# A four-layer convolution network: x2 made chunk by chunk, and the first two chunks' 7x7 products written to DRAM ahead of their factors

## The chip, the core and the metric

The kernel runs on one core of one Trainium2 chip. The metric is the device time of one execution in microseconds. The kernel before took 5029.39 us (median of 3 runs, 5021.53 to 5036.27). The engines are TensorE (PE, with its weight loads as PEld), VectorE (DVE), ScalarE (ACT), GpSimd (POOL) and SyncE (SP, which here only issues DMAs). Each runs its own queue of instructions in order, and waits for the others by semaphores.

## What is computed

The input is x of shape 4 x 384 x 64 x 64, float32. Four layers follow each other, each as x = x + layer(...). The change lies in the third and the fourth:

```
# layer 2, its end ("h1", "h2", token mixing done before; batch norms over batch and pixels)
h1 = gelu(bn(w1 @ tok));  h2 = bn(w2 @ h1);  ch = tok + h2
x2 = x + gate * ch + (1 - gate) * x_in

# layer 3, on v = groupnorm(x2) over 32 groups of 12 channels
avg, top = v.mean((2, 3)), v.max((2, 3))
x_w  = gelu(avg @ w_avg.T + b_avg + top @ w_max.T + b_max)      # one number per batch, channel
xr   = x_w * w_mix                                             # 7 x 7 taps per batch, channel
Nx   = norm(xr) / (norm(xr).mean over channels + 1e-6)
kern = gamma * xr * Nx + beta
out  = x2 + depthwise_conv7x7(v, kern)
```

For one batch and channel, kern is a factor times w_mix, plus beta. So out is x2, plus (gamma Nx x_w) times a 7x7 convolution of v with w_mix, plus beta times a 7x7 box sum of v. The convolution with w_mix is linear: the factor can be put on v before it, or on its result after it.

## The kernel before

The 384 channels are three chunks of 128 (j = 0, 1, 2); an image of a chunk is 128 partitions x 4096 floats, 2 MB. The phases follow each other: A to D make layers 0, 1 and the start of 2; E (part of `phase_ef`) makes the tokens and the first matrix product of layer 2, batch by batch in 4 blocks of 1024 pixels; F makes h2 by the second product; G (`phase_g`) does x2 and layer 3.

**E and F.** For each block, E loads three token tiles (L1363), scales them (L1364), multiplies (L1379) and stores the result, and the running sum "wx", to DRAM. Two token tiles rotate over two buffers; the third lies in a large buffer `z_`, in slot `i % 3` of 1024 floats. F loads, applies gelu (L1422), multiplies (L1435), copies to SBUF and stores h2 to DRAM, but for the last batch, whose h2 stays in `z_`. Statistics of the batch norms are gathered on DVE over all batches at the end (L1406, L1450).

**G, x2.** `x2_of(b)` makes one batch: for its three chunks (order 1, 2, 0) and quarters of 1024, ACT scales h2 into PSUM (L1614), DVE adds it to wx (L1615), ACT squares for the variance (L1617), DVE takes the maximum (L1618). Chunks 1 and 2 are stored to DRAM. Then come the factors of that batch: group norm, two small products on PE (L1636, L1653), gelu. Beside the next batch's x2, `first_chunk` makes chunk 0's strips and boxes of this one. Batch 3 comes first.

**G, strips and products.** `to_strips` (from SBUF, L1678) or `half_strips` (from DRAM, 64 channels at a time, L1555, L1561) apply the factor and norm, transpose on PE and lay the rows in `z`. `conv7(j, c0)` takes 8 channels: it loads weights (L1702), forms four Toeplitz blocks, two of three on DVE and one of three on POOL (L1709), multiplies on PE (L1722), adds the "rest" tile (L1730), which was loaded from DRAM (L1704), and stores the output (L1731). 16 such calls make a chunk, 48 in all.

**G, boxes.** `boxes(j, b, x)` adds beta times the box sum to x2: row sums on POOL (L1766, L1768) and DVE (L1769 to L1783), transposes and a product on PE (L1789, L1795), with an ACT copy between (L1791), and the scaled add into x2 on DVE (L1797). The result, x2 plus box, is the "rest" (L1801) that conv7 adds. So chunk j's boxes have to be done before its products; chunk 1's run beside chunk 0's products, chunk 2's beside chunk 1's, and none beside chunk 2's.

The order in which generators are advanced is written by hand in `phase_g`; a scheduler of the language then sets the final order on each engine. Buffers rotate by tag: two for weights, three each for "rest" and for x tiles, four for Toeplitz blocks.

Of the kernel before, what the change touches and what calls it, by code (L numbers as in the profile page):

```python
# [226 lines left out]
class _Builder:  # L227
    def __init__(self, ctx, tc, ins, out):
# [25 lines left out]
        self.rest = [self.dram.tile([P, 32, B, P], F32, tag=f"rest{j}", name=f"rest_{j}") for j in range(NJ)]  # L254
# [72 lines left out]
    def over_batches(self, name, mv):  # L327

        nc = self.nc
        st = self.sm([P, NJ, 6], f"{name}_st")  # L330
        m = self.sm([P, NJ, 2], f"{name}_m")
        for j in range(NJ):
            nc.vector.bn_stats(st[:, j, :], mv[:, j, :, 0])
            nc.vector.bn_aggr(m[:, j, :], st[:, j, :])
        within = self.sm([P, NJ], f"{name}_w")
        nc.vector.tensor_reduce(within, mv[:, :, :, 1], AX.X, ALU.add)
        var = self.sm([P, NJ], f"{name}_v")
        nc.vector.scalar_tensor_tensor(var, within, 1.0 / B, m[:, :, 1], ALU.mult, ALU.add)
        return m[:, :, 0], var
# [215 lines left out]
    def stats_tile(self, name):  # L555
        return self.sm([P, NJ, 8, 6], name, 1)
# [418 lines left out]
    def open_strips(self, ctx):  # L975
# [6 lines left out]
        self.h2_last = self.z_[:, 0 : NJ * N].rearrange("p (j n) -> p j n", n=N)  # L982
# [318 lines left out]
    x2_order = 1, 2, 0  # L1301

    def phase_ef(self, strips):
        tc, nc = self.tc, self.nc
        with ExitStack() as ctx:
# [47 lines left out]
            st = ep.tile([P, 6, B * 8, 6], F32, tag="h_st", name="h_st")  # L1353
            sums = cp.tile([P, NJ, B, 4], F32, tag="wx_sum", name="wx_sum")
            for b in range(B):
                for i in range(4):
                    blk = slice(i * 1024, (i + 1) * 1024)
                    t01 = io.tile([P, NJ - 1, 1024], F32, tag="tok", name="e_tok")
                    at = i % 3 * 1024
# [44 lines left out]
            mv = self.sm([P, 6, 2], "h_mv")  # L1404
            for o in range(6):
                nc.vector.bn_aggr(mv[:, o, :], st[:, o].rearrange("p a b -> p (a b)"))  # L1406
            a1, c1 = self.bn_scale_shift("bn_h", mv[:, :, 0], mv[:, :, 1], self.vec("cm_g1"), self.vec("cm_b1"))
# [8 lines left out]
            for b in range(B):  # L1416
                for i in range(4):
# [7 lines left out]
                    if b == B - 1 and 0 < i:  # L1425
                        j = self.x2_order[i - 1]
                        nc.sync.dma_start(self.x2_ahead[i - 1], self.wx[b][:, j])
                    for j in range(NJ):
                        out = self.h2_last[:, j, blk]
                        if b < B - 1:  # L1430
                            out = io.tile([P, 1024], F32, tag="x", name="f_h2")
# [12 lines left out]
                        if b < B - 1:  # L1444
                            nc.gpsimd.dma_start(self.h2[b][:, j, blk], out)
                for j in range(NJ):
                    nc.vector.bn_aggr(mvb[:, j, b], st2[:, j, 8 * b : 8 * b + 8].rearrange("p a b -> p (a b)"))
            mv = self.sm([P, NJ, 2], "h2_mv")
            for j in range(NJ):
                nc.vector.bn_aggr(mv[:, j, :], st2[:, j].rearrange("p a b -> p (a b)"))  # L1450
            a2, c2 = self.bn_scale_shift("bn_h2", mv[:, :, 0], mv[:, :, 1], self.vec("cm_g2"), self.vec("cm_b2"))
# [15 lines left out]
    def phase_g(self):  # L1467
# [8 lines left out]
        with ExitStack() as ctx:  # L1476
# [17 lines left out]
            sq = self.sm([P, NJ, 49], "mix_sq", 1)  # L1494
            nc.vector.tensor_mul(sq.rearrange("p j k -> p (j k)"), self.vec("w_mix"), self.vec("w_mix"))
# [3 lines left out]
            for k in ("a_s", "a_b", "b_s"):  # L1499
                setattr(self, k, cp.tile([P, NJ, B], F32, tag=k, name=k))  # L1500

            self.off = cp.tile([P, NJ, B, 3], F32, tag="off", name="off")


            self.z = self.z_[:, 0 : P * 136].rearrange("p (c k b) -> p c k b", k=34, b=B)
            nc.gpsimd.memset(self.z_[:, P * 136 :], 0.0)
            behind = iter(())
            for n, b in enumerate((B - 1, *range(B - 1))):
                for x in self.x2_of(b):
                    next(behind, None)  # L1510
                for _ in behind:
                    pass
                if n == 0:
                    nc.gpsimd.memset(self.z[:, :, 0], 0.0)
                behind = self.first_chunk(b, x)
            for _ in behind:
                pass
            self.pair_scales(cp)

            for j in range(NJ):  # L1520
                boxes = self.boxes_of(j + 1)
                for half in range(2):
                    strips = self.half_strips(j + half, 1 - half) if 0 < j + half < NJ else iter(())
                    for n in range(8):
                        self.conv7(j, 64 * half + 8 * n)
                        next(strips, None)
                        for _ in range(3 + n % 2):
                            next(boxes, None)
                    for _ in strips:
                        pass  # L1530
                for _ in boxes:
                    pass

    def pair_scales(self, pool):

        self.a_pair = pool.tile([P, 2, 2, NJ, 2], F32, tag="a_pair", name="a_pair")
        for half in range(2):
            for u in range(2):
                for k, v in enumerate((self.a_s, self.a_b)):
                    self.nc.gpsimd.dma_start(  # L1540
                        self.a_pair[64 * u : 64 * u + 64, k, half],
                        v[64 * half : 64 * half + 64, :, u::2],
                    )

    def half_strips(self, j, half):

        nc = self.nc
        for pair in range(2):
            for part in range(3):
# [10 lines left out]
                s, b = (self.a_pair[:, k, half, j, pair : pair + 1] for k in range(2))  # L1560
# [14 lines left out]
    def first_chunk(self, b, x):  # L1575
        yield from self.to_strips(0, b, x)
        yield from self.boxes(0, b, x)

    def boxes_of(self, j):
        if j < NJ:  # L1580
            for b in range(B):
                yield from self.boxes(j, b, self.load_x2(j, b))

# [8 lines left out]
    def x2_of(self, b):  # L1592


        nc = self.nc
        mv = self.sm([P, NJ, 2], "gn_mv")
        mx = self.sm([P, NJ], "max")
        for j in self.x2_order:
# [233 lines left out]
```

## Time and profile before

| what | value |
|---|---|
| median of 3 runs | 5029.39 us |
| the profiled execution | 5034.98 us |
| its span, first to last instruction | 5033.2 us |
| PE, DVE, ACT, POOL busy over the span | 92%, 54%, 42%, 15% |
| mean granted TensorE clock | 0.95 |
| moved by DMA | 723.30 MB |
| end of the last h2 product (F) | 4222.1 us |
| first 7x7 product | 4513.6 us |

The page cuts the span in 40 slices and gives each a digit: the busy share in tenths. "PEclk" is the TensorE clock granted, in tenths. A row of a group reads: line, engine, operation, written <- read, shape, count, then busy us and mean ns of one, then idle time just before and what ended it. A row of the table of stages gives, for each stretch of time, the busy time of PE, PEld, DVE, ACT and POOL with the number of instructions, then the clock, the mean busy share of the 16 DMA engines, and GB/s.

In phase G, DVE's largest groups are the Toeplitz blocks and the x2 work; ACT waits for DMA-loaded strips and for PE; the longest waits of PE lie between 4227 and 4510 us, for DVE's group norm and factors.

### The profile page before, as it was taken

To read this page: it belongs to the slowest core of one execution; us is meant where nothing else is said; L and a number is where in the kernel's file an instruction comes from. 1 tells how busy PE (TensorE), PEld (TensorE's weight loads), DVE (VectorE), ACT (ScalarE), POOL (GpSimd) and SP (SyncE) were. 2 spreads that over 40 slices of the span, in tenths; PEclk is the share of its full clock that TensorE was granted. 3 is DMA by queue.
4 is the path that set the end of the run, shared out by engine and by line. 5 is a ranking of instruction groups with operands and counts; after the bars stand their busy time and mean duration, and the time that the engine had idled before them with its cause. 6 is when DMAs were issued, how large, how long until landed. Compare 5 with 4: busy or idle time off the path is not lost. (4 is left out here: it accounts for less than half of the span.)

```text
span 5033.2 us, 47996 instructions
## 1 busy us (share of the span) xinstructions
PE 4607.7 (92%) x17875; PEld 2614.2 (52%) x17875; DVE 2729.0 (54%) x4480; ACT 2108.7 (42%) x2811; POOL 762.8 (15%) x568
## 2 busy tenths in 40 slices
PE   5999999999999999999988999699999996569999
PEld 2333444334443444435467888344444443558999
DVE  5322455644656445565867778544421114767775
ACT  4444344554445444445345665311133334652320
POOL 1000000000000000000035555000000000135543
PEclk8999999999999999999989999799999997569999
DMA  5210211110111101113259999766664433757876
GB/s 167 72 48 29 84 57 60 65 59 33 68 63 65 52 32 63 63 61 100 89 162 286 290 293 296 255 239 248 238 238 150 150 134 136 255 181 229 235 214 193
DMA packets 344919, 723.30 MB, mean 144 GB/s; under 512 B 22011, under 2 KB 172390, under 8 KB 337766
## 3 DMA queue, kind: packets, MB, share of 16 engines
q1 hardware_dynamic: 283032, 477.56, 30.4%
q0 software_dynamic: 33152, 136.60, 7.2%
q10 hardware_dynamic: 28494, 105.99, 5.4%
q8 instruction: 144, 2.36, 0.2%
q14 instruction: 97, 0.79, 0.0%
HBM read 432.48 MB, written 287.57 MB: 143 GB/s over the span
## 5 line engine op out<-in xcount | busy, mean ns | idle before, releaser
L749 PE MATMUL av<-probs,vt 128*128 128x512 f32 x2048 | 964.6, 606 | 0.0
L720 ACT ACTIVATE probs<-sc_s 128x1024 f32<-128x1024 f32 x512 | 500.9, 1021 | 788.1 <-PE av L749 781.5
L749 PEld LDWEIGHTS av<-probs,vt 128*128 128x128 f32 x2048 | 370.3, 192 | 468.1 <-issue 461.0
L1154 PE MATMUL conv_m<-toep,z 128*128 128x256 f32 x2304 | 522.2, 386 | 11.0 <-DVE toep L1135 6.8
L945 DVE SCALAR_TENSOR_TENSOR acc<-band,vecs,acc 128x512 f32<-128x512 f32 x708 | 496.7, 746 | 45.8 <-POOL band L906 40.0
L1435 PE MATMUL h_m<-f_h,cm_w_t 128*128 128x512 f32 x1152 | 496.4, 594 | 7.9 <-ACT f_h L1422 7.9
L1154 PEld LDWEIGHTS conv_m<-toep,z 128*128 128x128 f32 x2304 | 440.5, 193 | 73.1 <-DVE z L1087 4.9
L1379 PE MATMUL h_s<-e_tok,cm_w_t 128*128 128x512 f32 x768 | 367.4, 602 | 5.5 <-DVE e_tok L1364 5.5
L1435 PEld LDWEIGHTS h_m<-f_h,cm_w_t 128*128 128x128 f32 x1152 | 219.4, 191 | 284.9 <-issue 273.8
L1135 POOL TENSOR_TENSOR toep<-w,band 128x1536 f32<-128x1536 f32 x94 | 323.8, 3445 | 285.7 <-PE conv_m L1154 244.7
L1722 PE MATMUL conv_m<-toep,z 128*128 128x128 f32 x3072 | 366.4, 278 | 0.1
L1722 PEld LDWEIGHTS conv_m<-toep,z 128*128 128x128 f32 x3072 | 357.1, 194 | 0.5 <-issue 0.5
L712 PE MATMUL sc_s<-q,k 32*128 32x512 f32 x2048 | 297.8, 650 | 22.5 <-ACT probs L720 22.0
L868 PE MATMUL t_m<-w_in_t,xb 128*128 128x384 f32 x768 | 276.9, 495 | 2.7 <-DVE coef L885 1.6
L1386 ACT COPY e_h<-h_s 128x1024 f32<-128x1024 f32 x96 | 97.2, 1012 | 421.4 <-PE h_s L1379 421.4
L782 PE MATMUL proj_m<-xm,w_proj_t 128*128 128x512 f32 x576 | 265.9, 600 | 5.0 <-DVE xm L735 3.5
L1379 PEld LDWEIGHTS h_s<-e_tok,cm_w_t 128*128 128x128 f32 x768 | 148.1, 193 | 192.6 <-issue 185.6
L789 DVE SCALAR_TENSOR_TENSOR x_res<-proj_m,bn_c,x_res 128x512 f32<-128x512 f32 x96 | 71.8, 748 | 319.5 <-PE proj_m L782 316.5
L1388 DVE BATCH_NORM_STATS2 h_st<-e_h 128x6 f32<-128x512 f32 x192 | 123.4, 685 | 194.9 <-ACT e_h L1386 194.9
L1443 DVE BATCH_NORM_STATS2 h_st<-f_h 128x6 f32<-128x512 f32 x72 | 49.8, 694 | 323.1 <-ACT f_h L1442 323.1
L868 PEld LDWEIGHTS t_m<-w_in_t,xb 128*128 128x128 f32 x768 | 142.7, 191 | 138.8 <-issue 59.6
L1379 PE MATMUL h_s<-z,cm_w_t 128*128 128x512 f32 x384 | 198.0, 599 | 12.6 <-DVE z L1364 12.6
(369 smaller groups left out, 6285.1 us busy)
## 6 DMA issues: line engine op xcount, KB each, us to landing
d<-d_o ACTq DMA_DIRECT2D x96, 512.0 KB
c_d<-d SPq DMA_DIRECT2D x96, 512.0 KB
hid<-e_h ACTq DMA_DIRECT2D x16, 3072.0 KB
f_h<-hid SPq DMA_DIRECT2D x16, 3072.0 KB
x_in<-in_x SPq DMA_DIRECT2D x96, 256.0 KB
x_res<-in_x SPq DMA_DIRECT2D x32, 768.0 KB
xa<-x_res POOLq DMA_DIRECT2D x32, 768.0 KB, 3.7
xa_in<-xa SPq DMA_DIRECT2D x32, 768.0 KB
```

Source lines behind the costliest of these rows:

```text
L712: nc.tensor.matmul(s[:, g], lhsT=k4[32 * g : 32 * g + 32, c], rhs=q[i][32 * g : 32 * g + 32], start=True, stop=True,)
L720: nc.scalar.activation(p[:, h * 1024 : (h + 1) * 1024], s[:, 2 * h : 2 * h + 2].rearrange("p a b -> p (a b)"), AF.Exp, scale=0.25,)
L749: nc.tensor.matmul(av, lhsT=vt[:, 4 * c + v, :], rhs=p[:, v * 512 : (v + 1) * 512], start=c == 0 and v == 0, stop=c == 7 and v == 3,)
L782: nc.tensor.matmul(m, lhsT=self.w_proj[:, j, o * P : (o + 1) * P], rhs=xm[:, j], start=j == 0, stop=j == NJ - 1,)
L868: nc.tensor.matmul(m[:, 0:C], lhsT=xb[:, j], rhs=self.w_in[:, j, :], start=j == 0, stop=j == NJ - 1,)
L945: nc.vector.scalar_tensor_tensor(out, src(j, k), w, done, ALU.mult, ALU.add)
L1135: eng.tensor_tensor(t, self.w53[:, at : at + 192].rearrange("p (m n) -> p m n", n=8).unsqueeze(2).to_broadcast([P, 24, 8, 8]), band.rearra ...
L1154: nc.tensor.matmul(m[:, c * 256 : (c + 1) * 256], lhsT=self.z_[:, at : at + P], rhs=t[:, 12 * c + 4 * i : 12 * c + 4 * i + 4].rearrange("p ...
L1379: nc.tensor.matmul(s[:, v, :], lhsT=w1[:, j, o * P : (o + 1) * P], rhs=t[j][:, v * 512 : (v + 1) * 512], start=j == 0, stop=j == NJ - 1,)
L1388: nc.vector.bn_stats(st[:, o, 8 * b + 2 * i + v, :], h[:, o, v * 512 : (v + 1) * 512])
L1435: nc.tensor.matmul(m, lhsT=w2[:, o, j * P : (j + 1) * P], rhs=h[:, o, v * 512 : (v + 1) * 512], start=o == 0, stop=o == 5,)
L1722: nc.tensor.matmul(m[:, ch * P : (ch + 1) * P], lhsT=self.z_[:, at : at + P], rhs=t[:, 8 * c + 2 * i : 8 * c + 2 * i + 2].rearrange("p m a ...
```

## The change

It makes x2 for chunk 0 of all batches first, then its strips, scaled by 1 and with the group mean taken off (the mean is known ahead of x2 from the sums). Then chunk 0's products run and are stored raw, without their factor; beside them x2 of chunks 1 and 2 is made (in `phase_g` two or three steps of `x2` for each conv7). When all x2 are there, `factors` makes the factors of all batches at once. Chunk 1's strips are unscaled too and its products raw; chunk 2's strips carry the factor, as before. All boxes run beside the products of chunks 1 and 2, in the order (2, all batches), (0, all), (1, all), 4 or 5 steps for each conv7; for chunks 0 and 1 the box loads the raw products and adds them, times the factor, and stores the output itself. Chunk 0's x2 is now stored to DRAM and loaded back as well.

Besides: all h2 go to DRAM, the last batch's too; E's third token tile rotates over the batches; the statistics of both batch norms are kept by batch and joined by `over_batches`, which is rewritten; some small tiles move to other pools.

```diff
+        self.rest = self.dram.tile([P, 32, B, P], F32, tag="rest", name="rest")
+        self.raw = [self.dram.tile([P, P, P], F32, tag=f"raw{j}", name=f"raw_{j}") for j in range(NJ - 1)]
...
@@ over_batches
+        nc.vector.tensor_reduce(mean, mv[:, :, :, 0], AX.X, ALU.add)
+        nc.vector.tensor_scalar(mean, mean, 1.0 / B, None, ALU.mult)
+        d = self.sm([P, n, B], f"{name}_d")
+        nc.vector.tensor_sub(d, mv[:, :, :, 0], mean.unsqueeze(2).to_broadcast([P, n, B]))
+        nc.vector.tensor_mul(d, d, d)
+        nc.vector.tensor_add(d, d, mv[:, :, :, 1])
+        nc.vector.tensor_reduce(var, d, AX.X, ALU.add)
+        nc.vector.tensor_scalar(var, var, 1.0 / B, None, ALU.mult)
@@ phase_ef
-                    at = i % 3 * 1024
+                    at = (4 * b + i) % 3 * 1024
...
+                for o in range(6):
+                    nc.vector.bn_aggr(hmv[:, o, b], st[:, o, 8 * b : 8 * b + 8].rearrange("p a b -> p (a b)"))
...
-                        nc.sync.dma_start(self.x2_ahead[i - 1], self.wx[b][:, j])
+                        nc.sync.dma_start(self.x2_ahead[i - 1], self.wx[i - 1][:, 0])
...
-                        if b < B - 1:
-                            nc.gpsimd.dma_start(self.h2[b][:, j, blk], out)
+                        nc.gpsimd.dma_start(self.h2[b][:, j, blk], out)
@@ phase_g
+            self.group_means()
             behind = iter(())
+            for b in range(B):
+                for x in self.x2_of(0, b):
                     next(behind, None)
                 for _ in behind:
                     pass
+                behind = self.to_strips(0, b, x)
             for _ in behind:
                 pass
+            self.pair_scales(1)
...
+            x2 = others(*(self.x2_of(j, b) for j in (1, 2) for b in range(B)))
+            boxes = others(*(self.boxes(j, b) for j, b in ((2, 0), (2, 1), (2, 2), (2, 3), (0, 0), (0, 1), (0, 2), (0, 3))))
+            boxes1 = others(*(self.boxes(1, b) for b in range(B)))
             for j in range(NJ):
                 for half in range(2):
                     strips = self.half_strips(j + half, 1 - half) if 0 < j + half < NJ else iter(())
                     for n in range(8):
                         self.conv7(j, 64 * half + 8 * n)
                         next(strips, None)
+                        for k in range(5):
+                            if j == 0 and (k < 2 or k == 2 and n % 2):
+                                next(x2, None)
+                            if j == 1 or j == 2 and (k or n % 2):
+                                next(boxes, None)
                     for _ in strips:
                         pass
+                if j == 0:
+                    for _ in x2:
+                        pass
+                    self.factors()
+                    self.pair_scales(2)
+                if j == 1:
+                    boxes = others(boxes, boxes1)
...
+    def group_means(self):
+        m = self.over_groups("gn_pg", self.mean2)
+        nc.vector.tensor_copy(self.gm, m)
+        for i, k in enumerate((-6.0, -7.0, 2.0)):
+            nc.vector.tensor_scalar(self.off[:, :, :, i], self.gm, k, None, ALU.mult)
+        nc.gpsimd.memset(self.s_s, 1.0)
+        nc.vector.tensor_scalar(self.s_b, self.gm, -1.0, None, ALU.mult)
...
+    def factors(self):
...
+        nc.vector.tensor_mul(self.a_s, gx, r)
+        nc.vector.tensor_mul(self.b_s, over(self.vec("beta")), r)
+        nc.vector.tensor_copy(self.s_s[:, 2], self.a_s[:, 2])
+        nc.vector.scalar_tensor_tensor(self.s_b[:, 2], self.gm[:, 2], -1.0, self.a_s[:, 2], ALU.mult, ALU.mult)
@@ x2_of(j, b), the quarter
+            h = self.gw_p.tile([P, 1024], F32, tag="w7", name="g_h2", bufs=3)
+            nc.sync.dma_start(h, self.h2[b][:, j, sl])
+            for v in range(2):
+                m = self.pm("x2_m")
+                part = slice(q * 1024 + v * 512, q * 1024 + v * 512 + 512)
+                nc.scalar.activation(
+                    m, h[:, v * 512 : v * 512 + 512], AF.Identity, bias=at(self.g0), scale=at(self.gh)
+                )
+                nc.vector.tensor_add(x[:, part], x[:, part], m)
+            nc.scalar.activation(h, x[:, sl], AF.Square, bias=at(self.neg2), accum_out=self.x2_var[:, j, b, q : q + 1])
+            nc.vector.tensor_reduce(self.x2_max[:, j, b, q : q + 1], x[:, sl], AX.X, ALU.max)
+            yield None
+        nc.gpsimd.dma_start(self.scratch["x2"][b][j], x)
@@ conv7
-        nc.sync.dma_start(o, self.rest[j][c0 : c0 + 8].rearrange("c y b n -> (y b) c n"))
+        if j == NJ - 1:
+            nc.sync.dma_start(o, self.rest[c0 : c0 + 8].rearrange("c y b n -> (y b) c n"))
...
+        if j < NJ - 1:
+            nc.scalar.copy(of, m)
+            nc.scalar.dma_start(self.raw[j][:, c0 : c0 + 8], o)
+            return
         nc.vector.tensor_add(of, of, m)
         nc.sync.dma_start(self.out[j][:, c0 : c0 + 8], o)
@@ boxes
-            h = self.gw_p.tile([P, 16 * W], F32, tag="w7", name="box_7")
+            h = self.gw_p.tile([P, 16 * W], F32, tag="w7", name="box_7", bufs=3)
...
+            if j < NJ - 1:
+                d = self.gt_p.tile([P, 1024], F32, tag="rest", name="in_raw", bufs=3)
+                nc.sync.dma_start(
+                    d.rearrange("p (y n) -> p y n", n=P),
+                    self.raw[j].rearrange("(y b) c n -> c y b n", b=B)[:, 8 * part : 8 * part + 8, b],
+                )
+                xp = x[:, part * 1024 : (part + 1) * 1024]
+                nc.vector.scalar_tensor_tensor(xp, d, self.a_s[:, j, b : b + 1], xp, ALU.mult, ALU.add)
```

## The prediction

> **What bounds the kernel now.** I read the page first, then a table of stages, then the groups of the last stages by form. The page: TensorE (PE) is busy nearly everywhere, except in slices 34 to 36.
>
> ```profile
> span 5033.2 us, 47996 instructions
> ...
> PE   5999999999999999999988999699999996569999
> ...
> DVE  5322455644656445565867778544421114767775
> PEclk8999999999999999999989999799999997569999
> ```
>
> One digit is 126 us. The 6, 5, 6 lie between about 4150 and 4530 us; the granted clock falls there too. The table of stages (columns: PE, weight load, DVE, ACT, POOL busy, then clock, DMA share, GB/s) cuts this end in three: x2 with factors and chunk 0's strips and boxes; the 7x7 of chunks 0 and 1; the 7x7 of chunk 2.
>
> ```profile
> 4227.00:4510.00 283.00, 146.66 (x704) 132.83 (x705) 195.47 (x361) 188.12 (x264) 62.44 (x63) 0.57 0.62 223
> 4510.00:4890.00 380.00, 350.80 (x2962) 343.68 (x2963) 289.17 (x341) 105.73 (x187) 190.58 (x122) 0.97 0.76 225
> 4890.00:5033.00 143.00, 138.13 (x1237) 137.88 (x1235) 84.20 (x73) 14.96 (x19) 54.61 (x27) 1.00 0.65 198
> ```
>
> For 283 us no engine is the bound: DVE 69%, ACT 66%, PE 52% at a clock of 0.57. Then PE is the bound (92%, 97%), and DVE has room: 24% free in the second row, 41% in the third. The change moves 7x7 products (PE) into the first row and spreads DVE's boxes into the last. The first 7x7 matmul starts at 4513.6 us by the rows of its line, the last ends at 5028.2 by the chain. The groups by form, from 4215 us, give the prices:
>
> ```profile
> L1722 PE MATMUL conv_m<-toep,z 128*128 128x128 f32 x3072 | 366.4, 278 | 0.1
> ...
> L1709 DVE TENSOR_TENSOR toep<-wmix,band_p 128x1024 f32<-128x1024 f32 x129 | 155.5, 1215 | 42.6 <-PE conv_m L1722 35.7 <-issue 3.8 <-DMA wmix<-in_mix_t 1.9
> ...
> L1615 DVE TENSOR_TENSOR x<-x,x_m 128x1024 f32<-128x1024 f32 x48 | 57.4, 1214 | 13.6 <-ACT x_m L1614 12.3 <-DMA x<-wx 1.3
> L1618 DVE TENSOR_REDUCE x_max<-x 128x1 f32<-128x1024 f32 x48 | 57.3, 1211 | 0.0
> ...
> L1791 ACT COPY ht<-ht_m 128x512 f32<-128x512 f32 x96 | 56.1, 585 | 112.3 <-PE ht_m L1789 112.2
> ...
> L1797 DVE SCALAR_TENSOR_TENSOR in_x<-box_m,b_s,in_x 128x512 f32<-128x512 f32 x64 | 47.8, 747 | 22.0 <-PE box_m L1795 21.4
> ```
>
> The chain at the end shows 64 of these matmul records in 7.15 us, 0.1117 each: a chunk's 1024 cost 114 us of PE at full clock, 343 for three.
>
> **Phase E, a small part that is all on the path.** PE is the bound there, and the timeline shows it idle once at each change of batch:
>
> ```profile
> 3335.13 2.07 PE L1379 MATMUL h_s<-z,cm_w_t 128*128 128x512 f32 x2 [3.91 <-DVE z L1364]
> ...
> 3465.22 1.12 PE L1379 MATMUL h_s<-z,cm_w_t 128*128 128x512 f32 x2 [3.77 <-DVE z L1364]
> ...
> 3595.67 1.69 PE L1379 MATMUL h_s<-z,cm_w_t 128*128 128x512 f32 x2 [4.88 <-DVE z L1364]
> ```
>
> The third token chunk lives in slot i % 3: blocks 3 and 0 of adjoining batches take the same slot, so the load waits for the matmuls before it. With (4b + i) % 3 it has two blocks (62 us) of lead, as inside a batch, where no wait shows. Phase E ran from 3200.9 to 3717.8; 1152 records at 0.429 are 494; its cold start lost 3; 19.6 remain, 12.6 of it the idle above and the rest matmuls at half clock behind it. I take -19 (from -12.6 to -19.6). Statistics by batch add small DVE work under PE; at both ends of phase F one 0.96 us aggregate gives way to seven operations of some 0.16: nothing, within 0.5.
>
> **To the first x2.** The last h2 matmul, 4222.1, moves to 4203. Before, the first x2 used data kept in SBUF; now h2 is read back. Four DMAs of 0.4 us stand before that load on SP; a 512 KB store landed in 3.0 us; that ends about when the coefficients do (5.6 us after the last matmul). ACT starts at 4210; +3 at worst. The twelve extra h2 stores on POOL (12 x 3.0 = 36 us if bare) hide under batch 3's matmuls, as those of the other batches do.
>
> **Stage 1: x2 and strips of chunk 0 alone.** ACT carries it. x_m in halves of 512 costs 1.19 - 0.43 = 0.76 (0.43 is the 1024 copy's 1.01 less the 512 copy's 0.585). A tile: 8 x 0.76 + 4 x 1.33 (square and its accumulator) = 11.4; its strips 3 x 1.52 + 3 x (1.13 + 0.88) = 10.6. Four tiles: 88 us. DVE, beside it: 4 x (8 x 0.75 + 4 x 1.21) + 12 x 1.09 = 56. Before, ACT ran at 95 to 100% in such stretches (4240 to 4260): 93 us, the 7x7 starts at 4303 instead of 4513.6.
>
> **Stage 2: chunk 0's 7x7 beside the other eight tiles of x2.** PE: 114 + 6 strips x 1.2 = 121. DVE: 43 x 1.215 + 8 x 10.8 + 6 x 1.09 = 146. ACT: 8 x 11.4 + 16 raw copies x 1.01 + 16 DMA issues x 0.37 + 6 strips x 2.67 = 129. DMA: x2 in (6 tiles, two come early), h2 in (8) and x2 out (8), at 2.1 MB each 46 MB; raw out 8; weights 4; strips and first boxes 6: 64 MB. The full 10 us windows of the old x2 stage:
>
> ```profile
> 4290.00:4300.00 10.00, 4.69 (x21) 4.10 (x22) 7.57 (x14) 9.19 (x11) 1.97 (x3) 0.50 1.01 396
> ...
> 4370.00:4380.00 10.00, 5.05 (x39) 4.14 (x37) 9.00 (x9) 9.00 (x14) 0.55 (x1) 1.00 0.82 288
> ...
> 4390.00:4400.00 10.00, 7.23 (x34) 6.74 (x32) 8.99 (x21) 6.87 (x12) 2.69 (x2) 0.50 0.96 376
> ```
>
> At some 370 GB/s 64 MB need 173 us: DMA is the bound, not an engine. Two waits are new: ACT's raw copy waits for PE, with x_m and the squares of the next tile queued behind it (two product banks give it one step, 11 us, of slack); the weights' loads on SP wait for a finished step, with the h2 loads behind them (three h2 buffers cover some 17 us). I take 185; 155 if more is prefetched and DVE binds, 215 at 300 GB/s. The clock is a place where a rule speaks against the change. In the middle row PE was half busy and kept 1.00. The Trainium skill (TensorE: Matmul & The Clock Gate, "HAM oscillation") says that idle gaps over about 3.4 us halve the clock. A Toeplitz block is 1.79 us of matmuls and comes every 185/64 = 2.9 us, a gap of 1.1. At half clock throughout PE would need 242, 57 us more; but then it would have no gap. I follow the row.
>
> **Stage 3: chunk 1's 7x7, six of twelve boxes.** PE: 114 + 6 x 8 x 1.43 (0.44 transposes, 0.99 box matmuls in the chain) + 12 x 1.2 = 197. DVE: 52 + 6 x 18.8 (sum of the box rows over their tiles) + 13 + two tiles' adds, 10 = 188. PE binds; at the old 92%, 214. The factors come once for all batches instead of four times, but PE stands for part of the chain (two table loads of 1.28, 28 tiny matmuls, some 30 DVE operations); 25 product matmuls (5.6 us) stand between: +8 (0 to 15). Strips of chunk 2 and b_s wait for it, DVE's boxes behind these.
>
> **Stage 4: chunk 2's 7x7, six boxes.** DVE: 52 + 6 x 18.8 + 6 x 1.09 + 16 x 1.22 (the rest add, gone from the other 32 steps) + 24 new adds of raw products. That operation isn't in the trace; the nearest is a 1024 one of the same kind, 1.28 us (line 1393). But it has two SBUF operands, as has line 1779:
>
> ```profile
> L1779 DVE SCALAR_TENSOR_TENSOR box<-in_x,off,box x32: 609/740/2901, 4524.5 to 4871.9; 128x512 f32<-128x512 f32 x24, 128x384 f32<-128x384 f32 x8
> ```
>
> Median 740 ns, longest 2901, while a POOL block of 2.4 us runs. The skill (GPSIMD Engine Reference, "Key points") states that contention. By the median 24 adds are 31 us, with a full POOL block each 88; the row's mean (1.07) lies 0.33 over its median, so I take 1.6 each: 38. Sum 230, PE 191: DVE binds; at 94%, 245.
>
> **The sum.** 4303 + 185 + 214 + 8 + 245 + 5 (tail as before) = 4960; with the 1.8 outside the span 4962 against 5035.0 for the profiled run. That run lay 5.6 over the median: 4956, a gain of 73 us (1.5%). Of the 210 us by which the products start earlier, stage 2 takes back 185 - 114, the boxes and x2 work that now lie beside products the rest.
>
> **The rivals.** *Tighter packing* (0.2): phase C runs PE at 95% with DMA at 0.96 over 520 us; with stage 2 at 155 and stages 3 and 4 at 97% (204 + 237) the time is 4908. Against it: DVE and PE both above 85% in turn. *DMA saturated* (0.18): 512-byte pieces ran at 285 to 300 GB/s in phase C; stage 2 at 215 and stage 4 (some 60 MB) at 262 give 5003. *The ring of three "rest" buffers* (0.07), slower: in stage 4 they serve 16 rest tiles and 24 raw tiles, where before they served 16. Forty turns over three buffers in 245 us allow 18 us each from load to landed store. Before, 12.6 us a step allowed 38, and loads went out some 20 us ahead. A turn that takes 27 makes the stage 360: 5071. It decides from 25 us a turn; the time of before is reached at 24. A raw load that waits for a buffer stands on SP ahead of the weights of the next step and of the stores that free the ring. Against it: a load of 4, an add and a store of 4 fit in 18. That the change does nothing I exclude: in the order built, the first products stand right behind chunk 0's twelve strips.
>
> **How the numbers follow.** The likeliest case (0.55) is 4956, alone 4925 to 4985. With both rivals on the faster side the range is 4900 to 5003. 0.3%, 15 us, is about what a measurement here can tell: faster 0.90 (all but the ring and some of the saturated case), same 0.05, slower 0.05.
>
> **What would show it.** Products from about 4303 with no 4 us gap of PE in phase E; stage 2 some 185 us at a DMA share above 0.9 and a clock near 1; stage 3 PE above 90%; stage 4 DVE above 90%, adds near 1.6 us. Wrong if the clock stays at 0.5 beside x2, if SP stands for "rest" buffers, or if PE waits 30 us for the factors.

## The result, and the profile after

The changed kernel takes 4972.1 us (median of four runs, 4966.6 to 4979.7), the kernel before 5029.2 beside it: ratio 0.9888, 95% interval 0.9866 to 0.9910. That is 57 us less (45 to 67), where 73 were forecast; the time is 16 us above the forecast. The profiled run was the fastest of the four, 4966.6 us around a span of 4964.9, while that of before was one of the longer ones of its set (5035.0). So stages are compared here, not spans: some 10 us of the difference between the profiles lie ahead of phase E (E starts at 3191.3 us, before at 3200.9). That stretch varies by itself: in the variants of the changed kernel run below, which are alike up to there, E starts anywhere from 3190.0 to 3204.8 us. From E's start to the end the profiles differ by 58.7 us.

The page of the changed kernel, the same rows as shown of before:

```profile
span 4964.9 us, 47732 instructions
...
PE   5999999999999999998989999699999998677988
...
DVE  5322465644666445555867778655531112667898
...
PEclk9999999999999999998989999799999999699999
```

The low stretch of PE has moved one slice back, to slices 35 to 37, and is less deep. DVE now climbs to the end (6, 6, 7, 8, 9, 8), where before it fell. The table of stages (columns: PE, weight load, DVE, ACT, POOL busy, then clock, DMA share, GB/s): x2 and strips of chunk 0; chunk 0's products beside the other x2; chunk 1's products; chunk 2's.

```profile
4193.00:4289.00 96.00, 39.34 (x148) 26.97 (x146) 63.01 (x106) 83.50 (x110) 11.36 (x24) 0.52 0.80 286
4289.00:4484.00 195.00, 146.18 (x1172) 143.61 (x1173) 131.88 (x145) 114.83 (x167) 58.27 (x36) 0.89 0.95 332
4484.00:4728.00 244.00, 209.38 (x1729) 202.06 (x1729) 198.71 (x249) 92.89 (x166) 138.65 (x101) 0.97 0.66 208
4728.00:4958.00 230.00, 200.24 (x1648) 194.95 (x1646) 215.34 (x219) 48.37 (x98) 107.67 (x66) 0.96 0.73 250
```

4193 is the end of the last h2 matmul, 4289.1 the first product (before 4513.6), 4483.4 the start of the last x2 maximum, 4728.6 that of chunk 1's last raw copy. These four stretches are called stages 1 to 4, as in the forecast. The products start 224 us earlier and the kernel ends 68 earlier by the two profiles. Of the four rows the second is full by DMA (0.95), the first by ACT (87%; 97% from 4210 us, where the first x_m stands), the fourth by DVE (94%); in the third PE leads with 86%, under every figure that the forecast used. The groups by form, from 4193 us:

```profile
L1757 PE MATMUL conv_m<-toep,z 128*128 128x128 f32 x3072 | 392.8, 286 | 42.1 <-DVE toep L1744 19.2 <-POOL toep L1744 17.8 <-ACT g_h L1693 3.0
...
L1744 DVE TENSOR_TENSOR toep<-wmix,band_p 128x1024 f32<-128x1024 f32 x129 | 155.4, 1212 | 27.1 <-DMA wmix<-in_mix_t 16.6 <-PE conv_m L1757 8.6 <-issue 1.5
...
L1831 ACT COPY ht<-ht_m 128x512 f32<-128x512 f32 x96 | 55.9, 582 | 102.5 <-PE ht_m L1829 102.4
```

The products, which had waited 0.1 us in all, now wait 42, and 40.6 of it lie in stage 2: for Toeplitz blocks of DVE and POOL. The row that had been the pattern for the new add, and the new add (min/median/max ns):

```profile
L1819 DVE SCALAR_TENSOR_TENSOR box<-in_x,off,box x48: 605/740/2842, 4499.0 to 4929.6; 128x512 f32<-128x512 f32 x36, 128x384 f32<-128x384 f32 x12
```

```profile
L1847 DVE SCALAR_TENSOR_TENSOR in_x<-in_raw,a_s,in_x x32: 1271/1276/3433, 4662.4 to 4952.5; 128x1024 f32<-128x1024 f32 x32
```

Median 1276, longest 3433, mean 1.56 us (1.6 was taken). In phase E the waits of PE for z slots are gone; what is left are one wait at the start of E (h_s) and one at the start of F (h_m). The columns are us in total, times, longest:

```profile
PE h_m L1432 <- ACT f_h L1422: 8.7, 1, 8.7
PE h_s L1380 <- DVE e_tok L1365: 5.5, 1, 5.5
```

### The profile page after: what moved, and what is told of

It is laid out like the page before. It is cut to its first block, busy times and chain, and to the rows that moved or that the text cites. A ratio compares the mean times of both kernels' runs of the same rounds, so it can differ in the third digit from the quotient of the medians.

```text
span 4964.9 us, 47732 instructions
## 1 busy us (share of the span) xinstructions
PE 4552.7 (92%) x17665; PEld 2564.5 (52%) x17665; DVE 2769.8 (56%) x4438; ACT 2136.4 (43%) x2873; POOL 777.5 (16%) x593
## 2 busy tenths in 40 slices
DMA packets 346710, 752.64 MB, mean 152 GB/s; under 512 B 22779, under 2 KB 173158, under 8 KB 337510
## 4 chain that ended last, share of the span: by engine, by line
PE 45%; DVE 9%; DMA 4%; ACT 3%; issue 3%; POOL 1%; SPq 0%; ACTq 0%; DVEq 0%; POOLq 0%
PE h_s L1380 10%; PE h_m L1432 10%; PE conv_m L1156 9%; PE av L752 3%; PE t_m L871 2%; PE conv_m L1757 2%; DVE acc L948 2%; DMA wmix<-in_mix_t 1%; DMA g_h<-h 1%; PE out_m L966 1%; PE proj_m L785 1%; PE sc_s L715 1%; DVE toep L1744 1%; PE taps_m L941 1%; DVE toep L1137 1%
## 5 line engine op out<-in xcount | busy, mean ns | idle before, releaser
L1156 PEld LDWEIGHTS conv_m<-toep,z 128*128 128x128 f32 x2304 | 439.4, 193 | 71.0 <-DVE z L1089 4.9
L1757 PE MATMUL conv_m<-toep,z 128*128 128x128 f32 x3072 | 392.8, 286 | 42.1 <-DVE toep L1744 19.2
L1757 PEld LDWEIGHTS conv_m<-toep,z 128*128 128x128 f32 x3072 | 378.7, 202 | 44.4 <-POOL toep L1744 18.2
L1440 DVE BATCH_NORM_STATS2 h_st<-f_h 128x6 f32<-128x512 f32 x96 | 66.4, 694 | 429.1 <-ACT f_h L1439 429.1
```

The lines of the kernel that those rows point to most:

```text
L1156: nc.tensor.matmul(m[:, c * 256 : (c + 1) * 256], lhsT=self.z_[:, at : at + P], rhs=t[:, 12 * c + 4 * i : 12 * c + 4 * i + 4].rearrange("p ...
L1757: nc.tensor.matmul(m[:, ch * P : (ch + 1) * P], lhsT=self.z_[:, at : at + P], rhs=t[:, 8 * c + 2 * i : 8 * c + 2 * i + 2].rearrange("p m a ...
```

## The experiments

The theory: the gain is phase E's slots plus the laying of chunk 0's products beside the x2 work; DMA sets that stretch, DVE the end, and DVE is long there because it stands behind POOL at rows with two operands in SBUF. Against it: the overlap is worth little; the ring of three buffers sets the end; or round trips between the engines do, not any engine's busy time. Twelve kernels were run, each timed beside the kernel before (5023 to 5029 us); intervals are of that ratio. The changed kernel's is 0.9888 (0.9866 to 0.9910). Medians that lie 10 to 16 us from its 4972 have intervals that overlap this one, so they are read together with the stages of the profiles. Stage 4 is the steadiest: the changed kernel and the five runs that take no work out of it (the two that order x2, half of h2, and the two moved copies) have 234.2 to 236.3 us there.

**One line of the change in the kernel before.**

```diff
-                    at = i % 3 * 1024
+                    at = (4 * b + i) % 3 * 1024
```

> The kernel before with one line of the change: E's third token tile rotates by (4b + i) % 3. Theory: the three waits of PE at the changes of batch (12.6 us) and the half-clock matmuls behind them go, -19 us, some 5010. Rival: the next transfer in line (the two other token tiles, the x1 tile) ends just as late, and the gain is -5 us or less.

Measured: 5005.1 us, 0.9952 (0.9935 to 0.9968), 24 us less (16 to 33); the sum of the profile said 19, and in this run's profile E is 20.7 us shorter (504.0 against 524.7). The three waits are gone. This line is a third or more of the whole gain (19 to 24 of 57).

**x2 first, by program order.**

```diff
+            for _ in x2:
+                pass
             for j in range(NJ):
```

> The changed kernel with all twelve x2 tiles finished ahead of the first product; raw stores, late factors and boxes stay as they are. Theory (the gain is the overlap of products with x2): eight tiles alone take some 50 MB at 350 GB/s, 143 us, then chunk 0's products 125, against 195 for both together; less a shorter wait for the factors: +60 us, some 5030, all of G's gain gone. Rival (the gain comes from doing the factors once and from spreading the boxes): within +15, some 4985.

Measured: 4976.7 us, 0.9901 (0.9882 to 0.9921). The expectation missed because the edit didn't do what was meant. The timeline of its PE:

```profile
4287.36 2.61 PE L1722 MATMUL strip_m<-ident,ax 128*128 128x128 f32 x11 [1.34 <-ACT ax L1712]
4292.09 18.18 PE L1759 MATMUL conv_m<-toep,z 128*128 128x128 f32 x148 [2.12 <-ACT z L1729]
```

The products still start right behind the strips, at 4292 us; the last x2 maximum came at 4457 us instead of 4483, so the order written down moved x2 a little, but put nothing ahead of the products. The run says nothing on the worth of the overlap.

**x2 first, by data.** The band tables that every Toeplitz block is made from are multiplied by a 1.0 that hangs on the last x2 maximum.

```diff
+            for _ in x2:
+                pass
+            one = self.sm([P, 1], "one", 1)
+            nc.vector.tensor_scalar(one, self.x2_max[:, 2, 3, 3:4], 0.0, 1.0, ALU.mult, ALU.add)
+            for v in (self.band7_p, self.band7):
+                nc.vector.tensor_scalar(v, v, one, None, ALU.mult)
```

> The changed kernel with a real dependency put between the making of the x2 tiles of chunks 1 and 2 and chunk 0's products: the small band tables from which every Toeplitz block is made are multiplied by a number (1.0) that comes from the last x2 tile's maximum, so no product can start before the last of the eight x2 tiles is made. Output unchanged. Theory A (the gain comes from laying chunk 0's products, some 120 us of TensorE, beside the x2 work): the two stretches come one after the other, x2 alone about 145 us by its 48 MB of DMA and then the products 125 us or more, against 195 together: 60 to 80 us longer than the changed kernel, about 5040, no better than before. Rival B (the 195 us stretch is bound by DMA and the overlap is worth little): at most 15 us longer.

Measured: 5053.0 us, 1.0053 (1.0037 to 1.0069): 81 more than the changed kernel, and slower than before. Its timeline and its two stretches:

```profile
4427.00 1.98 PE L1659 MATMUL strip_m<-ident,ax 128*128 128x128 f32 x8 [137.26 <-DVE x L1697]
...
4433.10 12.10 PE L1763 MATMUL conv_m<-toep,z 128*128 128x128 f32 x87 [2.56 <-DVE toep L1750]
```

```profile
4289.00:4430.00 141.00, 3.05 (x14) 2.13 (x13) 81.27 (x99) 88.23 (x136) 10.27 (x13) 0.50 0.91 343
4433.00:4570.00 137.00, 134.56 (x1169) 133.99 (x1169) 76.01 (x70) 36.63 (x46) 63.65 (x34) 0.97 0.48 149
```

x2 alone takes 141 us with DMA at 0.91, chunk 0's products 137 us with PE at 98%: 278 against 195 together. The overlap is worth 81 us by the medians, 83 by these stretches and 73 by the profiles from E's start on; without it the changed kernel is slower than the one before, slots and all.

**Less for DMA.** Half of each h2 tile of chunks 1 and 2 is not loaded (the loaded half is used twice, so half of that h2 is left out).

```diff
-            nc.sync.dma_start(h, self.h2[b][:, j, sl])
+            if j == 0:
+                nc.sync.dma_start(h, self.h2[b][:, j, sl])
+            else:
+                nc.sync.dma_start(h[:, 0:512], self.h2[b][:, j, q * 1024 : q * 1024 + 512])
```

> The changed kernel, but for chunks 1 and 2 only the first half of each h2 quarter is loaded and used twice (half of that h2 is left out); every engine does the same work, DMA moves 8.4 MB less beside chunk 0's products. Theory (DMA is the bound of that stage): -8.4 MB at 370 GB/s, -20 us, some 4952. Rival (DVE or the waits between engines are the bound): within 5 us of 4972.

Measured: 4959.1 us, 0.9863 (0.9846 to 0.9879), 13 less. The rows of the x2 maximum, of this kernel and then of the changed one, give the place:

```profile
L1697 DVE TENSOR_REDUCE x_max<-x x48: 1172/1211/1220, 4221.5 to 4472.1; 128x1 f32<-128x1024 f32 x48
```

```profile
L1694 DVE TENSOR_REDUCE x_max<-x x48: 1175/1214/1221, 4212.2 to 4483.4; 128x1 f32<-128x1024 f32 x48
```

First to last maximum: 251 us against 271. The 8.4 MB that are missing take 25 us at 332 GB/s, and 20 come off; only loads were taken away, so DMA bound that stretch. At the end of chunk 1, 17 of the 20 us are left.

**POOL's Toeplitz blocks left out.** A constant block stands in for every third one, so a third of the products is made without its weights. The edit also gives the other blocks three buffers in place of four.

```diff
             on_pool = (c0 // 2 + pair) % 3 == 2
+            if on_pool:
+                t = self.const_t
+            else:
...
```

> The changed kernel without GpSimd's share of the Toeplitz blocks (every third block is left out: TensorE reads a constant block in its place, so a third of the 7x7 products has wrong weights; all other work stays). Theory A (the last two stages are set by VectorE, which stands for GpSimd at the same operands): VectorE's box rows fall back towards their durations of before (L1809's 1185 ns towards 750), and the time falls by 25 us (15 to 40). Rival B (the last two stages are set by round trips between TensorE, ScalarE and VectorE, not by busy time): 0 to 8 us less, though the box rows get shorter.

Measured: 4934.3 us, 0.9815 (0.9792 to 0.9838), 38 less. From the first raw copy to the last it takes 422 us (429 in the changed kernel), from there to the end 209 (236). DVE's rows by form in stage 4 (count | busy us, mean ns | idle before), of the changed kernel and then of this one:

```profile
L1847 DVE SCALAR_TENSOR_TENSOR in_x<-in_raw,a_s,in_x 128x1024 f32<-128x1024 f32 x24 | 38.9, 1621 | 0.1
...
L1809 DVE TENSOR_TENSOR box<-box,box 128x512 f32<-128x512 f32 x19 | 22.1, 1177 | 2.3 <-POOL box L1808 2.3
L1815 DVE SCALAR_TENSOR_TENSOR box<-in_x,off,box 128x384 f32<-128x384 f32 x20 | 19.8, 990 | 0.0
...
L1819 DVE SCALAR_TENSOR_TENSOR box<-in_x,off,box 128x512 f32<-128x512 f32 x15 | 17.4, 1158 | 0.0
L1814 DVE SCALAR_TENSOR_TENSOR box<-edge,off,box 128x128 f32<-128x128 f32 x15 | 14.9, 995 | 0.0
```

```profile
L1851 DVE SCALAR_TENSOR_TENSOR in_x<-in_raw,a_s,in_x 128x1024 f32<-128x1024 f32 x24 | 31.1, 1295 | 0.1
...
L1813 DVE TENSOR_TENSOR box<-box,box 128x512 f32<-128x512 f32 x19 | 17.0, 903 | 1.3 <-POOL box L1812 1.3
L1819 DVE SCALAR_TENSOR_TENSOR box<-in_x,off,box 128x384 f32<-128x384 f32 x20 | 12.2, 608 | 0.0
L1823 DVE SCALAR_TENSOR_TENSOR box<-in_x,off,box 128x512 f32<-128x512 f32 x15 | 11.1, 741 | 0.0
L1818 DVE SCALAR_TENSOR_TENSOR box<-edge,off,box 128x128 f32<-128x128 f32 x15 | 5.9, 393 | 0.0
```

The same five operations cost 113 us beside POOL's blocks and 77 without: 36 us of DVE's busy time in this stage go with POOL's blocks. The rows that have one operand in PSUM did not change (the add of the box matmuls 743 ns, the Toeplitz blocks 1.21 us).

**The raw adds left out**, all but 8 of their 1024 columns (the loads stay; chunks 0 and 1 lack their 7x7 part).

```diff
-                nc.vector.scalar_tensor_tensor(xp, d, self.a_s[:, j, b : b + 1], xp, ALU.mult, ALU.add)
+                nc.vector.scalar_tensor_tensor(xp[:, 0:8], d[:, 0:8], self.a_s[:, j, b : b + 1], xp[:, 0:8], ALU.mult, ALU.add)
```

> The changed kernel with the scaled add of the raw products cut to 8 of its 1024 columns (32 adds of 1.56 us on VectorE are left out, their DRAM loads and waits kept, so chunks 0 and 1 lack their 7x7 part). Theory A (VectorE's busy time sets stages 3 and 4): 32 x 1.56 = 50 us of VectorE go, 24 of the adds in stage 4 and 8 in stage 3, and the time falls by 35 to 45 us. Rival B (round trips, or TensorE at 87% of stage 4): 0 to 15 us less. Rival C (the ring of three shared buffers): buffers come free earlier by the adds' durations alone, 5 us less.

Measured: 4961.1 us, 0.9865 (0.9839 to 0.9891): 11 less, where "DVE binds" alone meant 35 to 45. Stage 4 has the same DVE relief as the run before, and gains 9 us instead of 27. Its row, then that of the run without POOL's blocks:

```profile
4741.00:4968.00 227.00, 197.54 (x1642) 193.13 (x1640) 179.43 (x217) 49.54 (x98) 102.23 (x67) 0.95 0.74 249
```

```profile
4733.00:4942.00 209.00, 191.08 (x1644) 187.45 (x1641) 178.72 (x219) 49.59 (x98) 58.63 (x45) 0.99 0.81 279
```

DVE 179 in both, so DVE's busy time is not what sets 227 against 209. What is, stays open. POOL holds its own box adds and blocks in one queue here (102 against 59 us), and PE's waits are 24 us in all against 12; but in the chain of work that ended last in this stage POOL's rows have only some 10 us. It has some 69 us of DVE, 57 of PE and 55 of DMA, 27 of them loads of raw products. In the changed kernel the same chain has some 112 us of DVE, 62 of PE and no DMA among its longer pieces. So DVE led there, and loads seem to have been next once the adds were gone.

**Both cuts together.**

> The changed kernel without GpSimd's Toeplitz blocks and without the raw adds (both cuts of the two earlier runs in one: a third of the 7x7 products has wrong weights, and chunks 0 and 1 lack their 7x7 part). VectorE's work in stage 4 falls to about 145 us. Theory (TensorE, 191 to 200 us busy in stage 4, stands right behind VectorE, so that relief of VectorE alone soon ends at it): stage 4 stays at 200 to 209 us, and the time is 0 to 12 us below the run without the blocks alone (4934). Rival (VectorE's chain still sets stage 4 at 209): the adds' 24 x 1.3 = 31 us come off nearly in full, 25 us or more less than 4934.

Measured: 4925.8 us, 0.9808 (0.9792 to 0.9825), 8.5 under the run without blocks by the medians and 9.3 by the profiles from E's start on, though the intervals of the ratios overlap.

```profile
4721.60:4925.00 203.40, 191.91 (x1642) 188.76 (x1640) 152.69 (x216) 49.83 (x98) 50.53 (x46) 0.98 0.81 278
```

Stage 4 is 203 us with PE at 94%: with DVE at 75% and POOL at 25%, PE is what is left to set it, and the rival's 25 us or more are ruled out. The changed kernel's 236 lie 33 above that.

**Work moved off DVE.** In the strips, the middle copy too goes to ACT:

```diff
-                    if i == 1:
-                        nc.vector.tensor_copy(zv.rearrange("p c k b -> p k b c"), mv)
-                    else:
-                        nc.scalar.copy(zv, mv.rearrange("p k b c -> p c k b"))
+                    nc.scalar.copy(zv, mv.rearrange("p k b c -> p c k b"))
```

> The changed kernel with the DVE third of the strip copies (half_strips, 24 of 1.08 us, 18 of them beside chunks 1 and 2) moved to ACT, which is 28% busy there. Theory (DVE is the bound of the last two stages): -15 to -20 us, some 4955. Rival (PE is the bound): within 5 us of 4972, or later by the longer chain of three copies on one engine.

Measured: 4972.2 us, 0.9891 (0.9874 to 0.9907): nothing, though DVE's total fell by 26 us. In the last two stages PE's wait for ht copies on ACT (ht is the boxes' copy between transpose and product) rose from 36 to 51 us (that for the strips' copies there fell from 17 to 10): so part of what left DVE's queue seems to have come back as waiting in that of ACT.

**A copy moved off ACT**, because ht copies are queued behind it:

```diff
-                nc.scalar.copy(s[:, 0:2], last[:, 8:10])
+                nc.gpsimd.tensor_copy(s[:, 0:2], last[:, 8:10])
```

> The changed kernel with one of the boxes' copies, the two carried rows of box_2 (24+ copies of 128x256, the line on which ScalarE stands 92 us in the last two stages for VectorE's read of the buffer), put on GpSimd, which is the buffer's next writer anyway. Output unchanged. Theory B (TensorE's waits for ht copies queued behind that copy on ScalarE, 36 us in 22 waits in the trace, are what lengthens stages 3 and 4): 8 to 20 us less. Theory A (VectorE's busy time sets them): 0, or up to 5 us more through GpSimd's added work.

Measured: 4976.8 us, 0.9903 (0.9880 to 0.9927): not faster. Stage 4 is 235.4 us, against 236.3 without the edit. But the wait was moved more than taken away: ACT now stands for DVE's box rows at the next copies of the boxes (L1788, L1793), 84 us in stage 4 against 95, and PE's waits for ht copies in the last two stages fell only from 36 to 34 us. So theory B is not refuted by this run; it was hardly tested.

**The ring with two buffers** in place of three (both uses of the tag).

```diff
-        o = self.gt_p.tile([P, 8, P], F32, tag="rest", name="rest_o", bufs=3)
+        o = self.gt_p.tile([P, 8, P], F32, tag="rest", name="rest_o", bufs=2)
```

> The changed kernel with two shared buffers in place of three for the products' results, the rest loads and the raw loads. Output unchanged. By the rival of the prediction (every use of the ring costs a turn of loads, adds and stores, and the ring sets the pace): stage 4 has 16 rest loads and 24 raw loads, 40 uses; with three buffers at its pace, two would make it 3/2 as long, over 100 us more. By the theory (VectorE and TensorE set the pace and the ring waits for them): waits of DMA in the trace are 37 us in 13 waits, and 0 to 25 us more.

Measured: 4987.6 us, 0.9922 (0.9893 to 0.9951), 15 more. Stage 4 grew only from 236 to 241 us, stages 2 and 3 from 429 to 442. Two buffers for 40 uses in 241 us allow 12 us a turn, so a turn is well under the 25 us from which the forecast's slower rival decides. More buffers than three were not tried.

**POOL's blocks given to DVE in chunks 1 and 2**, and then the strips' copies to ACT as well:

```diff
-            on_pool = (c0 // 2 + pair) % 3 == 2
+            on_pool = j == 0 and (c0 // 2 + pair) % 3 == 2
```

> The changed kernel with GpSimd's third of the Toeplitz blocks given to VectorE in chunks 1 and 2 (42 blocks of 1.21 us); in chunk 0, where DMA binds, GpSimd keeps its share. Output unchanged. Theory (what GpSimd's blocks cost is VectorE's wait behind them, 37 us of box rows and raw adds in stage 4 by the run without these blocks, and GpSimd's box adds queued behind them): stage 4 trades 21 x 1.21 = 25 us more against 37 less, 12 us less on VectorE, and GpSimd's queue is free for the boxes: 10 to 20 us less than the changed kernel. Rival (the wait behind GpSimd is small; the gain of the run without blocks came from the missing work): VectorE gets 51 us longer over two stages in which it is over 90% busy, 15 to 40 us more.

Measured: 4961.6 us, 0.9874 (0.9847 to 0.9901), 10 less by the medians and by the profiles from E's start on; the two intervals overlap.

> As the run before (Toeplitz blocks of chunks 1 and 2 on VectorE alone), and besides the strips' 24 copies of 1.08 us taken from VectorE to ScalarE (0.58 us there), which by themselves changed nothing. Output unchanged. Theory (VectorE and TensorE are the two near bounds of stages 3 and 4, 216 and 200 of 236 us in stage 4, and a relief of one is cut short by the other): VectorE falls by another 6.5 us in stage 4 and 6.5 in stage 3, 0 to 10 us less than the run before. Rival (ScalarE's queue, with the ht copies in it that TensorE waits for, becomes the limit): 5 us more.

Measured: 4956.4 us, 0.9857 (0.9826 to 0.9888), the fastest version that leaves nothing out; its runs (4944 to 4960) and those of the changed kernel (4967 to 4980) don't overlap, though the intervals of the ratios do; from E's start on its profile is 20 us shorter. In stage 4 of the first of the two, DVE has 21 blocks more (25 us) and is 8 us less busy:

```profile
L1744 DVE TENSOR_TENSOR toep<-wmix,band_p 128x1024 f32<-128x1024 f32 x62 | 74.1, 1210 | 3.6 <-DMA wmix<-in_mix_t 3.6
...
L1809 DVE TENSOR_TENSOR box<-box,box 128x512 f32<-128x512 f32 x20 | 13.7, 703 | 0.0
```

Stage 4 of the first, then of the second:

```profile
4720.00:4955.50 235.50, 203.91 (x1642) 194.81 (x1640) 207.71 (x244) 50.20 (x100) 57.02 (x47) 0.95 0.72 251
```

```profile
4723.50:4950.30 226.80, 199.77 (x1642) 192.84 (x1640) 198.56 (x237) 52.11 (x106) 55.77 (x46) 0.95 0.75 259
```

In the first it is nearly as long as without the edit, 235.5 against 236.3; of the 9.4 us by which the profile is shorter, 7.6 lie in stages 2 and 3 (421.7 against 429.3). Stage 4 itself gets shorter, by 9.5 us, only with the copies moved as well. So what POOL's blocks cost in DVE's busy time is shown; where on the path each part of it lands is not.

## Why the prediction was right, and where it was off

The mechanism and the sign held: products of chunk 0 beside x2, DMA the bound of that stage, and the whole forecast of the total within 16 us. Part of that closeness is luck, since misses in stages 3 and 4 partly cancelled. By its own steps:

- **Phase E, -19.** From E's start to F's start 505.6 us against 524.7, 19.1 less. The run of the line alone gives 24 (16 to 33).
- **Stage 1.** 96 us from the last h2 matmul to the first product; the forecast had 100 (4203 to 4303).
- **Stage 2, 185: measured 195.** DMA binds, as said, and the bytes were right, 64 MB; the rate was mis-sized. 370 GB/s, taken from full windows of the old stage, gave 173 us; the 185 that was taken comes to some 346 GB/s. 332 were measured, which gives the 10 us. The DMA part of this window's page:

```profile
DMA packets 12201, 64.69 MB, mean 332 GB/s; under 512 B 1456, under 2 KB 1456, under 8 KB 10288
```

  The two new waits are there, but not quite as described. ACT's raw copies waited only 7 us for PE. On SP the longest wait is that of h2 loads (L1684) for a buffer that ACT's squares still hold, with the weights' loads (L1735) behind them; the forecast had it the other way round:

```profile
SPq L1684 <- ACT g_h L1693: 107.5, 27, 15.7
SPq L1735 <- DVE toep L1744: 12.1, 4, 7.7
```

  The timelines of ACT, DVE and PE at one place show how late loads reach PE:

```profile
4474.27 1.48 ACT L1688 ACTIVATE x_m<-g_h,g,gh 128x512 f32<-128x512 f32 x2 [7.57 <-DMA g_h<-h]
```

```profile
4475.08 1.39 DVE L1691 TENSOR_TENSOR x<-x,x_m 128x512 f32<-128x512 f32 x2 [7.86 <-ACT x_m L1688]
4478.78 1.22 DVE L1744 TENSOR_TENSOR toep<-wmix,band_p 128x1024 f32<-128x1024 f32 x1 [2.31 <-DMA wmix<-in_mix_t]
```

```profile
4480.15 8.22 PE L1757 MATMUL conv_m<-toep,z 128*128 128x128 f32 x46 [9.51 <-DVE toep L1744]
```

  Read from the last line up: PE waits 9.5 us for a block. On DVE that block stands behind an x2 add, which waits for ACT, which waits for an h2 load; then it waits 2.3 us more for its own weights, a load too. An average DMA share of 0.95 reaches PE like this, through in-order queues.
- **The clock.** 0.89 over stage 2, where half clock throughout had meant 242 us. The forecast set its row against the clock rule that it quotes, but the two agree here. PE had five waits over 4 us in this stage (4.5, 5.8, 8.5, 9.3 and 9.5 us), and after the first 6 us, which still had the half clock of stage 1, only around these did the clock fall to half, for 3.4 to 10 us each; at waits under 3 us it stayed at 1.00. The last of them, in windows of 10 us:

```profile
4460.00:4470.00 10.00, 8.68 (x78) 8.49 (x77) 6.62 (x8) 6.09 (x8) 2.37 (x1) 1.00 0.97 408
4470.00:4480.00 10.00, 0.65 (x6) 0.46 (x5) 2.60 (x4) 3.81 (x5) 2.54 (x2) 0.79 1.07 289
4480.00:4490.00 10.00, 9.85 (x63) 9.88 (x64) 6.52 (x11) 6.16 (x12) 7.80 (x6) 0.69 1.01 414
```

  In stage 4 the clock also fell three times, for 3.4 us each, at waits of 2.0 to 2.5 us, so the length of one wait is not all that counts. In the serial run, PE idle for 137 us, the clock of that stretch was 0.50.
- **Stages 3 and 4, together 472: measured 481.** The division was off, 222 + 250 forecast (with the tail) against 244.6 + 236.3. Six and six box tiles were counted. Five calls a step over sixteen steps are 80, at twelve to a tile 6.7 tiles, and the trace has 29 of the 48 quarters in stage 3 (19 stand in stage 4, in L1809's row above):

```profile
L1809 DVE TENSOR_TENSOR box<-box,box 128x512 f32<-128x512 f32 x29 | 34.5, 1190 | 12.4 <-POOL box L1808 12.4
```

  Five quarters are, at the forecast's own prices, some 24 us of DVE and 14 of PE. Moved from stage 4 to stage 3 they would make the forecast 237 + 225 (an estimate from its terms), 462 in place of 472: closer in each stage, farther in the sum. So the count explains a part only, and its error hid another. The rows of DVE add up to 451 us (218 + 233) where 418 were forecast: the box rows of twelve tiles are 255 us, not 12 x 18.8 = 226. DVE's busy time is yet 415, because neighbouring rows overlap by some 0.1 us each, and the forecast took its sum of rows for busy time: two misses that cancel. PE's work was 21 under (388, 409). What failed is "PE above 90%" in stage 3: it was 86%, DVE 81%. In stage 4 DVE was at 96% up to 4925 us (188.8 of 196.4), but the experiments show that "DVE binds" says too much: 37 us less of DVE brought 9, the strips' copies nothing. PE's busy time is only 8% under DVE's. Whether the boxes' way through ACT, POOL, DVE and PE is as long as either was not measured.
- **The factors' bubble, +8.** PE waited 0.9 us for the factors themselves. The 60 us from 4484 on have PE at 81%, which the bubble, DVE's 9 us of waits inside the factors' chain and the start of the boxes share; these were not told apart.
- **The ring.** One sign that the forecast names for being wrong did appear: in stage 4 SP stood some 108 us at the loads into the ring (55 at "rest", 53 at raw products). It decides little here, since taking one of the three buffers away lengthened this stage by 5 us only.
- **The add, 1.6 us.** 1.62 in stage 4, and 1.30 without POOL's blocks, which agrees with the contention that the Trainium skill states (GPSIMD Engine Reference, "Key points"). The forecast put it into the new add by estimate; for the box rows it took 18.8 us of DVE a tile from before, and they rose as well (L1809 from 752 to 1185 ns in the mean), since more of them now lie beside POOL's blocks.

The terms on the profiled path: -4 in stage 1, +10 in stage 2, +9 in stages 3 and 4, against the forecast's own: 15 too low, as the median was (16). One slip in its rivals changes nothing: 262 us for a saturated stage 4 doesn't follow from 60 MB at 285 to 300 GB/s, which are 200 to 211.

**Where the expected gain went.** The products start 224 us earlier, but the work that filled that time is not gone, it lies beside them now. By the runs: the overlap is worth 73 to 83, the slots 19 to 24, together 92 to 107; 57 are left. So the change's price for them is 35 to 50 us by subtraction: 32 adds (11 of it by the run without them), boxes and adds that moved into an end without slack, and more DMA. The last is less than the raw products suggest. Their 16.8 MB written and as much read take the place of the same bytes of "rest" for chunks 0 and 1; the whole kernel moves 29.3 MB more (752.64 against 723.30), by sizes 12.6 for the h2 of the last batch and 16.8 for chunk 0's x2, each written and read back. The price was not measured part by part.

## What to carry to other kernels

Laying a PE stage beside a stage that only DMA and ACT fill can be worth up to the shorter of the two (here 73 to 83 us of 137); how much is read from the DMA bytes of both, at the rate of mixed traffic, not of the best windows. Before an engine is called the bound of a stage, ask how far behind the next one is: here DVE led by 8%, and taking 37 us from it brought 9. A block that POOL makes "for free" cost DVE time here at the rows with two SBUF operands beside it; look at the rows' longest against their median.

## What the runs showed that was not expected

- POOL's 2.4 us blocks make a short DVE operation beside them two and a half times as long: L1814 (128x128) takes 995 ns in the mean with them and 393 without.
- TensorE's granted clock was at 0.50 through the 141 us of the serial run in which PE was 2% busy, and 1.00 in the window from 4443 us, ten after that run's first product (4433.1); beside x2 it held 0.89 with PE busy 75% of the time.
- Moving the program's text (x2 drained first) left the first product where it was, right behind the strips, and brought the end of x2 forward by 27 us; only a data dependency put x2 ahead of the products.
